# A LayerNorm-attention kernel: the first group in halves, x loaded ahead of the weights, a plain first slice, and two small moves in every group

**Chip, cores, metric.** One core of one Trainium2 chip. The metric is the device time of one execution in microseconds (us).

## The reference

128 graphs of 128 nodes with 768 features; 12 heads of 64; everything is fp32.

```python
h = jnp.maximum(_layernorm(x), 0.0)                       # no gain, no offset, eps 1e-5
q, k, v = (split_heads(h @ W + b) for W, b in ((Wq, bq), (Wk, bk), (Wv, bv)))
scores = jnp.einsum('bhqd,bhkd->bhqk', q, k) / 8
scores = scores + beta * adj[:, None]
scores = jnp.where(adj[:, None] > 0, scores, -9e15)
x = x + merge_heads(softmax(scores) @ v)
```

## The kernel before

It works in 32 groups of four graphs. In each group the three projections run as three "slices" (`qk0`, `v`, `qk1`). A slice multiplies a 2x3 by a 3x3 grid of blocks with 15 block products in place of 18. For that it needs sums of activation blocks (`S..`, 11 per group) and sums of weight blocks (`T..`, 15 per slice, once for the whole kernel). The 15 products write into four PSUM banks (chains a to d); a product that adds to a bank may not start until VectorE or ScalarE has taken the bank's last result out (an *eviction*).

The parts that the change and the argument touch, with cuts marked `# ...`:

```python
def load_x(G, g):                       # 4 DMAs on the sync queue
    # ...
        nc.sync.dma_start(t[a * SQ:(a + 1) * SQ], src[a])
for g in range(GRP):
    load_x(0, g)
# load_weights("qk0"): 18 DMAs on the scalar queue, at the same time
#     nc.scalar.dma_start(t[:, :, i * P:(i + 1) * P], part(w, oc * P, P))

def sum_weights(sl, n):                 # one T block
    # ... the two "-" sums: nc.vector.scalar_tensor_tensor
        e = nc.gpsimd if n % 3 == 2 else nc.vector
        e.tensor_tensor(wt[sl, name], wt[sl, a], wt[sl, b], ALU.add if sign > 0 else ALU.subtract)

def moments_2(G, mean, d):
    nc.tensor.matmul(pm[G][:, 1], mean8.rearrange("p a i -> p (a i)"), d, start=True, stop=True)
    nc.vector.tensor_reduce(ve, pm[G][:, 1], AX.X, ALU.add)
    nc.vector.tensor_scalar(ve, ve, EPS, None, op0=ALU.add)
    nc.gpsimd.tensor_tensor(rstd[G], ve, nhalf.to_broadcast([P, GRP * NB]), ALU.pow)
    nc.vector.scalar_tensor_tensor(shift[G], mean, -1.0, rstd[G], op0=ALU.mult, op1=ALU.mult)

def norm(G, g):                         # ScalarE: x <- relu(rstd * x + shift)
def to_hT(G, r, k):                     # VectorE transposes: one A block from x
def sum_acts(G, n):                     # one S block; every third on GpSimd

def make_bias(G, raw):
    # ... transpose, mask kp, a = min(beta*adj, cap)
    nc.gpsimd.tensor_tensor(t, a, a, ALU.mult)
    nc.vector.tensor_reduce(bm, t, AX.X, ALU.max)
    nc.vector.tensor_tensor(seen_b, seen_b, bm, ALU.max)
    nc.gpsimd.memset(t, MASKED)
    nc.vector.copy_predicated(t, kp, a)

# the eviction in slice v, in product():
    nc.vector.tensor_tensor(o4, bias..., p..., ALU.add)      # first into a v tile
    nc.vector.tensor_tensor(o, o, got, ALU.add)              # later ones

# the start: all of group 0's statistics, norm, transposes and sums, then the first product
moments_2(0, *moments_1(0))
for g in range(GRP): norm(0, g)
for n in HT_ORDER: to_hT(0, int(n[1]), int(n[2]))
for n in range(len(SUMS_A)):
    sum_acts(0, n); sum_weights("qk0", n)
# ... make_bias(0, a)
for G in range(NG):
    # group 0: the sums of v's weights under slice qk0, those of qk1 under slice v
    slice_of(G, "qk0", todo)
    # statistics, moments, bias and norm of group G+1 under slice v
    slice_of(G, "v", todo)
    # to_hT and sum_acts of group G+1, attention of group G under slice qk1
    slice_of(G, "qk1", todo)
```

## Time and profile before

| | before |
|---|---|
| time, median of 3 runs | 3209.32 us (3209.32 to 3209.43) |
| span of the profiled run, granted clock | 3208.3 us, 0.997 |
| TensorE busy | 3109.2 us, 97% |
| first product of slice qk0, of v, of qk1 in group 0 | 52.71, 82.71, 111.84 us |
| one group from the next (power to power) | 97.96 us |

TensorE is busy nearly all the time, so a change counts by the idle time it takes from TensorE. A row of the waits gives the engine that stood still, the tile and line it was about to work on, what it waited for, and then microseconds in all, number of times, longest. A row of the timeline gives start, length, engine, line, operation, output<-inputs, shape, count, and in brackets the idle time before it and what ended it. The lines themselves stand in the prediction. A product is four matmuls in the program; the trace records each of them as two, so a product is x8. Line numbers are those of each kernel's own text: the product is L305 before and L314 after.

### The profile page before, as it was taken

How to read it: one execution, taken by the hardware profiler on the slowest of the kernel's cores; microseconds unless marked ns; L12 is line 12 of the kernel's file. 1: busy time of each engine (PE TensorE's matmuls, PEld its weight loads, DVE VectorE, ACT ScalarE, POOL GpSimd, SP SyncE). 2: the span in 40 equal slices, each digit the busy share in tenths (PEclk: the TensorE clock that was granted, in tenths of full speed). 3: DMA queues.
4: the chain of work that ended last, by engine and by line, in shares of the span. 5: the costliest groups of instructions: out<-in, count | busy, mean ns of one | idle time of the engine just before them, and what ended most of it. 6: DMA issues, size and time to landing. Idle time of an engine off the chain costs nothing.

```text
span 3208.3 us, 46341 instructions
## 1 busy us (share of the span) xinstructions
PE 3109.2 (97%) x17794; PEld 2737.0 (85%) x17794; DVE 1962.6 (61%) x5031; ACT 781.5 (24%) x1665; POOL 571.2 (18%) x448
## 2 busy tenths in 40 slices
PE   3999999999999999999999999999999999999998
PEld 2888888888888888888888888888888888888887
DVE  6665566655666655666566666556665666665554
ACT  1222122222132221222221322222222213222221
POOL 3111111111111111111111111111111111111110
PEclk9999999999999999999999999999999999999998
DMA  6111121112111211211121112112111112121111
GB/s 153 43 52 45 53 63 46 53 43 56 53 54 49 54 43 53 63 47 53 45 55 53 55 48 56 41 53 63 47 53 46 54 53 56 47 56 37 50 40 31
DMA packets 358385, 169.94 MB, mean 53 GB/s; under 512 B 84368, under 2 KB 358032, under 8 KB 358160
## 3 DMA queue, kind: packets, MB, share of 16 engines
q1 hardware_dynamic: 344064, 159.45, 18.2%
q10 hardware_dynamic: 14096, 7.48, 0.9%
q8 instruction: 142, 2.33, 0.3%
q14 instruction: 83, 0.68, 0.1%
HBM read 116.53 MB, written 50.33 MB: 52 GB/s over the span
## 4 chain that ended last, share of the span: by engine, by line
PE 87%; DVE 5%; POOL 3%; issue 1%; DMA 1%; ACT 1%; ACTq 0%; POOLq 0%; DVEq 0%
PE pc_qk L305 18%; PE pb_qk L305 14%; PE pa_qk L305 14%; PE av L357 10%; PE pd_qk L305 7%; PE sc L344 7%; PE pb_v L305 5%; PE pc_v L305 5%; PE pa_v L305 3%; PE pd_v L305 3%; POOL rstd L243 3%; DVE A L258 2%; DVE v L321 2%; ACT x L251 1%; DMA v_B<-in_L_gnn_Wv_dram 0%
## 5 line engine op out<-in xcount | busy, mean ns | idle before, releaser
L251 ACT ACTIVATE x<-x,shift,rstd 128x192 f32<-128x192 f32 x512 | 227.8, 533 | 902.8 <-DVE shift L245 902.8
L348 ACT ACTIVATE e<-e 128x512 f32<-128x512 f32 x384 | 235.6, 630 | 819.9 <-DVE e L347 819.9
L368 POOL TENSOR_TENSOR xo<-xo,o 128x512 f32<-128x512 f32 x192 | 244.2, 1272 | 974.6 <-DVE seen L366 608.6
L357 PEld LDWEIGHTS av<-v,e 128*128 128x128 f32 x3072 | 375.4, 193 | 15.4 <-ACT e L348 5.4
L305 PE MATMUL pb_qk<-S,qk_T 128*128 128x256 f32 x1536 | 373.0, 386 | 0.5 <-DVE qk L330 0.5
L357 PE MATMUL av<-v,e 128*128 128x65 f32 x3072 | 367.0, 273 | 4.7 <-ACT e L348 4.7
L305 PEld LDWEIGHTS pb_qk<-S,qk_T 128*128 128x128 f32 x1536 | 281.7, 190 | 41.6 <-DVE qk L330 0.9
L347 DVE SCALAR_TENSOR_TENSOR e<-sc,biasT 128x512 f32<-128x512 f32 x384 | 246.6, 684 | 104.1 <-PE sc L344 104.1
L330 DVE TENSOR_TENSOR qk<-qk,pb_qk 128x512 f32<-128x512 f32 x256 | 174.4, 681 | 179.8 <-PE pb_qk L305 166.2
L326 ACT ACTIVATE qk<-pc_qk,bqk 128x256 f32<-128x256 f32 x384 | 160.9, 470 | 489.3 <-PE pc_qk L305 489.3
L258 DVE STREAM_TRANSPOSE A<-x 128x256 f32<-128x256 f32 x384 | 222.0, 618 | 77.7 <-ACT x L251 41.3
L305 PE MATMUL pc_qk<-S,qk_T 128*128 128x256 f32 x1024 | 243.8, 381 | 16.1 <-DVE S L264 16.1
L305 PE MATMUL pa_qk<-S,qk_T 128*128 128x256 f32 x1024 | 248.5, 385 | 0.0
L305 PE MATMUL pc_qk<-S,qk_B 128*128 128x256 f32 x1024 | 248.5, 385 | 0.0
L305 PEld LDWEIGHTS pc_qk<-S,qk_T 128*128 128x128 f32 x1024 | 195.6, 191 | 43.0 <-DVE S L264 16.2
L344 PE MATMUL sc<-qk 64*128 64x128 f32 x3072 | 224.4, 285 | 0.0
L305 PEld LDWEIGHTS pa_qk<-S,qk_T 128*128 128x128 f32 x1024 | 189.4, 190 | 30.8
L305 PEld LDWEIGHTS pc_qk<-S,qk_B 128*128 128x128 f32 x1024 | 189.4, 190 | 30.8
L344 PEld LDWEIGHTS sc<-qk 64*128 64x128 f32 x3072 | 187.1, 188 | 30.1 <-issue 21.2
L330 DVE TENSOR_TENSOR qk<-qk,pd_qk 128x512 f32<-128x512 f32 x128 | 88.0, 687 | 181.2 <-PE pd_qk L305 181.2
L264 POOL TENSOR_TENSOR S<-S,A 128x512 f32<-128x512 f32 x64 | 81.8, 1278 | 642.4 <-PE pa_qk L305 614.2
L305 PE MATMUL pb_v<-v_T,S 128*128 128x256 f32 x768 | 184.7, 383 | 5.4 <-DVE v L321 5.4
(106 smaller groups left out, 4647.2 us busy)
## 6 DMA issues: line engine op xcount, KB each, us to landing
x<-in_x_dram SPq DMA_DIRECT2D x512, 96.0 KB, 2.2
xo<-in_x_dram SPq DMA_DIRECT2D x192, 256.0 KB, 2.8
out_dram<-xo SPq DMA_DIRECT2D x192, 256.0 KB, 2.2
adj<-in_adj_dram SPq DMA_DIRECT2D x128, 64.0 KB, 2.3
qk_B<-in_L_gnn_Wq_dram ACTq DMA_DIRECT2D x18, 128.0 KB, 3.7
qk_B<-in_L_gnn_Wk_dram ACTq DMA_DIRECT2D x18, 128.0 KB, 3.6
v_B<-in_L_gnn_Wv_dram ACTq DMA_DIRECT2D x9, 256.0 KB, 5.9
bv_b<-in_L_gnn_bv_dram ACTq DMA_DIRECT2D x1, 384.0 KB, 4.7
```

The costliest lines, as they stand in the source:

```text
L243: nc.gpsimd.tensor_tensor(rstd[G], ve, nhalf.to_broadcast([P, GRP * NB]), ALU.pow)
L251: nc.scalar.activation(t, t, AF.Relu, bias=shift[G][:, n:n + 1], scale=rstd[G][:, n:n + 1])
L258: nc.vector.transpose(t[:, :, g * N:(g + 1) * N].rearrange("p c (b i) -> p c b i", i=SQ), src)
L264: e.tensor_tensor(t, A[G, a], A[G, b], ALU.add if sign > 0 else ALU.subtract)
L305: nc.tensor.matmul(p[:, i, :], lhs, rhs, start=(first and i == 0 and c == 0), stop=(c == 1), skip_group_check=True)
L326: nc.scalar.activation(t[:, i, :], p[:, i, :], AF.Identity, bias=bqk[:, i, oc:oc + 1], scale=float(sign))
L330: nc.vector.tensor_tensor(t, t, p, ALU.add if sign > 0 else ALU.subtract)
L344: nc.tensor.matmul(ps[i][:, g, :], t[r, 1, at], t[r, 0, at], start=True, stop=True)
L347: nc.vector.scalar_tensor_tensor(e, ps[i], SCORE_CAP * ISCALE, biasT[G], op0=ALU.min, op1=ALU.add)
L348: nc.scalar.activation(e, e, AF.Exp, scale=1.0 / ISCALE)
L357: nc.tensor.matmul(pa[:, 2 * g + i, :], es[G, oc, i][:, 2 * r + g, :], vt[G, "v", r, h // 4][:, 4 * g + h % 4, :], start=True, stop=True)
L368: nc.gpsimd.tensor_add(t, t, o.rearrange("p a (b j) d -> p (a b) (j d)", j=2))
```

## The change

Its intent: let TensorE start as soon as half of x is there, and make the block sums while it already works. Group 0 is treated in two halves; x is loaded first on two queues and the weights behind it; slice qk0 of group 0 is computed plainly with 18 products, which needs no sums; the sums of v and qk1 are to be made under it, and those of qk0 (for the groups after, all but two of them on GpSimd) under slice v. In all groups the LayerNorm shift moves from VectorE to GpSimd (with a mean already negative), and the bias is made in two steps, so that VectorE need not wait for GpSimd's square.

The diff, cut to its core (left out: a new order of the weight sums, five of which now overwrite a raw weight block, and a few small loads and scalings on other queues):

```diff
-            nc.sync.dma_start(t[a * SQ:(a + 1) * SQ], src[a])
+            engines[a % len(engines)].dma_start(t[a * SQ:(a + 1) * SQ], src[a])
-        load_x(0, g)
+        load_x(0, g, (nc.sync, nc.scalar))
-    nc.vector.tensor_scalar(mean8, ..., 0.125, None, op0=ALU.mult)
+    made = nc.vector.tensor_scalar(mean8, ..., -0.125, None, op0=ALU.mult)
-                nc.scalar.dma_start(t[:, :, i * P:(i + 1) * P], part(w, oc * P, P))
+                nc.sync.dma_start(t[:, :, i * P:(i + 1) * P], part(w, oc * P, P))
 # moments_2 (now over blocks lo to hi of the group)
-        nc.vector.scalar_tensor_tensor(shift[G], mean, -1.0, rstd[G], op0=ALU.mult, op1=ALU.mult)
+        shifted = nc.gpsimd.tensor_tensor(t, mean, r, ALU.mult)
 # bias_1
-        nc.gpsimd.tensor_tensor(t, a, a, ALU.mult)
-        ... tensor_reduce(bm, t, ...), tensor_tensor(seen_b, seen_b, bm, ALU.max)
         nc.gpsimd.memset(t, MASKED)
         nc.vector.copy_predicated(t, kp, a)
+        nc.gpsimd.tensor_tensor(a, a, a, ALU.mult)
+    def bias_2(G, a):
+        ... tensor_reduce(bm, a, ...), tensor_tensor(seen_b, seen_b, bm, ALU.max)
+    def plain_slice(G, sl, todo):        # 6 blocks x 3 products of raw A and B blocks
+    def after(f, *args):                 # queue behind the last transpose / the last shift
+        with tc.issue_after(first["dve"].ins), tc.issue_after(first["pool"].ins):
+            return f(*args)
+    with tc.issue_after(made.ins):
+        for step in range(3):
+            half(0, step)                # statistics, moments, norm, transposes of half 0
 # loop, group 0
+            with tc.issue_after(first["dve"].ins):
+                half(1, 0)
+            then(1, lambda: half(1, 1))
+            then(3, lambda: half(1, 2))
+            for n in range(len(SUMS_A)):
+                then(n + 5, lambda n=n: after(sum_acts, 0, n))
+            for n in range(len(SUMS_B)):
+                then(n // 2 + 5, lambda n=n: after(sum_weights, "v", n))
+                then(n // 3 + 13, lambda n=n: after(sum_weights, "qk1", n))
+            then(9, lambda: bias_2(0, after(bias_1, 0, adj_0)))
+            plain_slice(0, "qk0", todo)
 # under slice v of group 0
+                then(n, lambda n=n: after(sum_weights, "qk0", n, nc.gpsimd))
```

## The prediction

> **What bounds the kernel now.** I read the page first, then the waits of TensorE, the chain of work in order of time, and the timeline of the start and of one later group. TensorE is the bound: it is busy in nearly all of the span, so only its idle time and its extra matmuls count.
>
> ```profile
> PE 3109.2 (97%) x17794; PEld 2737.0 (85%) x17794; DVE 1962.6 (61%) x5031; ACT 781.5 (24%) x1665; POOL 571.2 (18%) x448
> ...
> PE pm L227 <- DVE st L219: 31.9, 1, 31.9
> PE pa_v L305 <- DVE v L321: 27.1, 31, 0.9
> PE pc_qk L305 <- DVE S L264: 16.1, 1, 16.1
> PE pb_v L305 <- DVE v L321: 5.4, 31, 0.2
> PE pm L238 <- DVE dev L233: 3.5, 1, 3.5
> ```
>
> Waits are in us: total, times, longest. Two stocks are on offer. One is the start: three waits that occur once, 31.9 + 3.5 + 16.1 = 51.5 us. The other recurs in each of 31 groups: 27.1 + 5.4 = 32.5 us. If the change won both, 84 us would be 2.6%.
>
> The recurring wait, in the timeline of a late group (start, length, engine, ...):
>
> ```profile
> 2549.95 2.90 POOL L243 TENSOR_TENSOR rstd<-ve,nhalf 128x16 f32<-128x16 f32 x1 [16.23 <-DVE ve L241]
> 2552.89 0.17 DVE L245 SCALAR_TENSOR_TENSOR shift<-mean,rstd 128x16 f32<-128x16 f32 x1 [3.08 <-POOL rstd L243]
> 2553.10 7.12 ACT L251 ACTIVATE x<-x,shift,rstd 128x192 f32<-128x192 f32 x16 [28.65 <-DVE shift L245]
> 2554.99 1.17 DVE L258 STREAM_TRANSPOSE A<-x 128x256 f32<-128x256 f32 x2 [1.33 <-ACT x L251]
> 2556.78 1.99 PE L305 MATMUL pa_v<-v_B,S 128*128 128x256 f32 x8 [0.88 <-DVE v L321]
> ```
>
> The power on GpSimd, then the shift, then four norm instructions on ScalarE, then two transposes on VectorE, which stand in VectorE's queue ahead of the eviction that TensorE needs.
>
> The start, in the chain of work (start, length, what):
>
> ```profile
> 52.71 3.78 PE pc_qk L305 x8
> 56.49 2.35 PE pa_qk L305 x8
> 58.84 1.73 PE pb_qk L305 x8
> ...
> 88.81 1.99 PE pc_v L305 x8
> ...
> 111.84 1.73 PE pc_qk L305 x8
> ```
>
> A product is four matmuls, 1.73 us when warm. The first slice starts at 52.71. At 88.81 stands the fourth product of the second slice (v), at 111.84 the first of the third (qk1). From there on both kernels have the same TensorE order; the rest lasts 3208.3 - 111.8 = 3096.5 us.
>
> **What the Trainium skill says.** "SBUF — State Buffer", section "SBUF: two separate sides": VectorE and GpSimd share a port pair, an exclusive lock held for a whole instruction, which a VectorE operation with two SBUF inputs needs against a GpSimd operation that reads SBUF; the other blocks. The trace agrees:
>
> ```profile
> 34.15 1.75 POOL L198 TENSOR_TENSOR v_T<-v_T,v_B 128x512 f32<-128x512 f32 x1 [2.23 <-DVE v_T L198]
> 34.69 1.25 DVE L233 SCALAR_TENSOR_TENSOR dev<-st,dev 128x32 f32<-128x32 f32 x1
> ...
> 50.84 2.94 POOL L264 TENSOR_TENSOR S<-A,A 128x512 f32<-128x512 f32 x2 [6.52 <-DVE A L258]
> 51.72 3.21 DVE L264 TENSOR_TENSOR S<-A,A 128x512 f32<-128x512 f32 x3
> ```
>
> A 128x32 operation, 0.2 us elsewhere, lasts 1.25 and ends with the sum on GpSimd. In the second pair five sums last from 50.84 to 54.93, 4.09 us, close to 2 x 1.27 + 3 x 0.6 = 4.3: one at a time, taking turns. "TensorE: Matmul & The Clock Gate", Part 1: after an idle window of some 3.4 us the array runs at half clock, and warms in about that time. The trace agrees: 3.78 and 2.35 after 16 us of idle, so 3.78 + 2.35 - 2 x 1.73 = 2.67 us lost. "GPSIMD Engine Reference", section 3.1: a GpSimd tensor_tensor of 2048 elements takes 4497 ns; with 1270 ns for 512 in this trace I estimate a fixed part of 0.2 us.
>
> **The change part by part.**
>
> 1. *x ahead of the weights, on two queues.* Before, both streams share the DMA engines, and the last x piece lands at 29. The 2 us stretches show 241 to 269 GB/s from 2 to 14 us. The first half of x is 0.79 MB: at 250 GB/s from about 1.7 us, landed at about 5. Two batches of statistics on VectorE (1.1 each) end at 6.3. Then the moments: matmul 0.65, four small operations 0.9, matmul 0.65, two small 0.5, the power. The power took 2.9 for 16 columns; for 8 I take 1.6. Shift on GpSimd 0.3. Norm of two batches 3.6 (16 took 7.12), last transpose 0.6. Sum: TensorE starts at 15.5 instead of 52.7. The weights follow from 6 us, 2.36 MB at 250 GB/s, and stay ahead of it.
>
> 2. *Plain first slice.* 18 products for 15: 18 x 1.73 + 2.67 cold + 0.3 for moments = 34.1, so it ends at 49.6. Its tenth product needs the second half of x. The built order puts that half's moment matmuls after products 2 and 4 (21.7 and 25.2); then 0.5 + 1.6 + 0.3 + 3.6 + 0.6 gives 32.0, and TensorE asks at 34. It fits, by 2 us.
>
> 3. *The sums under it.* This is where I think the gain goes. Before, the sums of two weight slices and of the activations ran while TensorE waited anyhow. Now nearly all three slices' sums stand in VectorE's and GpSimd's queues after the last transpose, at 33, and the built order has 31 VectorE sums and the bias work *ahead of* the first eviction of slice v. Among them two wait for GpSimd; the later, T1 of qk1, for the twentieth GpSimd operation after that time. The lock makes these additive: 20 GpSimd operations x 1.13 (1.27 less what is dispatched while waiting) = 22.6, VectorE's 27 sums x 0.55 and four others 1.5 = 16.3, from 33.8: 72.7. Then three more sums, one or two GpSimd turns, three statistics and the eviction, 4.5 to 5.5: 78. TensorE gets through three products of slice v (49.6 + 5.2 = 54.8) and then stands still, because the fourth adds to the bank that the eviction must read first. That is a wait of about 23 us, and long enough to go cold: another 2.67.
>
> So the fourth product starts at 78 instead of 88.8. The rest of the slice took 111.8 - 88.8 = 23.0 before; with the cold start 25.7, and perhaps 0.7 for the bias of the next group, which now stands between its last evictions: qk1 starts at 104.5 instead of 111.8. Gain: 7.3 us.
>
> 4. *Shift on GpSimd, negative mean.* In the built order each later group is the same on TensorE and VectorE except for the shift and the bias steps. VectorE no longer waits for the power, but it was idle for another 1.33 us afterwards for ScalarE, so nothing is released: the transposes still wait for norm, norm for shift, shift for the power. Before, 0.25 us pass from the power's end to ScalarE's start; with a GpSimd shift of 0.2 and two hand-overs about 0.3. Cost: 31 x 0.08 = 2.5 us.
>
> 5. *Bias in two steps.* It takes a 1.15 us wait of VectorE for GpSimd out of each group. TensorE does not wait there: 0.
>
> Sum: 3209.3 - 7.3 + 2.5 = 3204.5. I put 3203, as the rivals below weigh on the fast side.
>
> **Rivals.** (a) *The sums hide.* Were there no lock, VectorE would reach the eviction at 33 + 31 x 0.6 + 4.1 = 56, TensorE would wait 2 us, and qk1 would start near 79: a gain of 30 us, 3180. For it speaks that the order was evidently chosen so; against it the two pairs above. In between, VectorE may win the lock more often, yet it still has to wait for those 20 GpSimd operations. (b) *The recurring wait goes*, 32.5 us more: 3170 or, with (a), 3147. Against it: the 1.33 us of waiting for ScalarE after the shift, and an unchanged order. (c) *The shift on GpSimd is slow*, or the small power is not cheaper: 0.3 us per group is 9 us, and a power of 2.9 for 8 columns moves part 1 by 1.3 and the sums with it by 2.6. Then 3212. (d) The second half of x is late: a few us inside the first slice, which the wait at the fourth product would absorb.
>
> **Range and chances.** The firm limit is the start: with everything hidden 37.2 - 5.2 = 32 us, 1.0%. To be faster by 2% (64 us) needs (a) and (b) together, which I hold for nearly excluded; slower by 2% would need 2 us lost in every group, and nothing in the order does that. The low end, 3187, is two thirds of the way to (a); the high end, 3212, is (c).
>
> **What would show it.** Right: the first product at 15 to 17 us; in slice v of group 0 one TensorE wait of 18 to 26 us for an eviction (v), with VectorE and GpSimd busy in turns beneath it and VectorE sums of 1.6 us instead of 0.68; the wait of pa_v for v still 31 times 0.9; steady groups 97.97 to 98.1 us apart, as before (power to power). Wrong: no such wait (the lock costs less than I think), a recurring wait gone, or groups closer together than 97.9.

## The result, and the profile after

The changed kernel is correct and took 3204.72 us (median of 4, 3204.31 to 3205.04), against 3209.38 us (4 runs) of the kernel before on the same chip. The ratio is 0.9985 with a 95% interval of 0.9968 to 1.0002: the same within 2%. A ratio is the mean time of one kernel's fast runs over that of the other's fast runs of the same rounds, so it is not quite the ratio of the medians.

| | before | after |
|---|---|---|
| span of the profiled run, clock | 3208.3 us, 0.997 | 3203.1 us, 0.993 |
| first product of group 0 | 52.71 | 16.92 |
| first product of slice v | 82.71 | 50.62 |
| first product of slice qk1 | 111.84 | 103.82 |
| from there to the end of the span | 3096.5 | 3099.3 |
| power to power | 97.96 | 98.05 |

TensorE starts 35.8 us earlier and reaches slice qk1 only 8.0 us earlier; then it loses 2.8 us in the rest. The page of the kernel after, TensorE's busy time:

```profile
PE 3115.6 (97%) x17822; PEld 2743.3 (86%) x17822; DVE 1963.9 (61%) x4988; ACT 781.2 (24%) x1665; POOL 590.1 (18%) x489
```

It is 6.4 us busier than before, of which three more products at 1.73 us are 5.2. TensorE's waits in the kernel after:

```profile
PE pa_v L314 <- DVE v L330: 29.6, 31, 1.0
PE pc_v L314 <- DVE v L325: 23.5, 1, 23.5
PE pm L227 <- DVE st L218: 7.9, 1, 7.9
PE plain L404 <- DVE A L263: 6.9, 1, 6.9
PE pb_v L314 <- DVE v L330: 5.1, 30, 0.2
```

The three single waits of the start (51.5 us) have become 7.9 + 6.9 + 0.9 us, and one new wait of 23.5 us stands in slice v. The recurring pair has grown from 32.5 to 34.7 us. The timeline has TensorE's first product of the kernel after:

```profile
16.92 5.79 PE L404 MATMUL plain<-A,qk_T 128*128 128x256 f32 x16 [6.86 <-DVE A L263]
```

The chain of work of the kernel after, around the new wait and at the start of qk1:

```profile
77.89 0.79 DVE st L218 x3
78.68 0.60 DVE v L325
79.42 3.53 PE pc_v L314 x8
82.94 1.73 PE pd_v L314 x8
...
103.82 1.73 PE pc_qk L314 x8
```

The fourth product of slice v starts at 79.42, as soon as VectorE has got to the eviction (v) at 78.68; it runs at half clock (3.53 for 1.73 us). What VectorE and GpSimd did until then, in the timeline of the kernel after:

```profile
52.19 0.68 DVE L270 TENSOR_TENSOR S<-A,S 128x512 f32<-128x512 f32 x1
...
61.21 1.59 POOL L198 TENSOR_TENSOR qk_T<-qk_T,qk_T 128x512 f32<-128x512 f32 x1
61.60 1.74 DVE L270 TENSOR_TENSOR S<-A,S 128x512 f32<-128x512 f32 x1
62.76 1.70 POOL L198 TENSOR_TENSOR qk_T<-qk_T,qk_B 128x512 f32<-128x512 f32 x1
63.27 1.75 DVE L198 TENSOR_TENSOR qk_T<-qk_T,qk_B 128x512 f32<-128x512 f32 x1
```

The sum at 52.19 has VectorE to itself and lasts 0.68 us. From 61 us on each engine's operation starts before the other's has ended and cannot finish until it has: 1.74 and 1.70 us, with 1.67 us from one VectorE sum to the next (61.60 to 63.27). That is what the prediction expected to see. Last, a late group of the kernel after, which answers to the five lines of before:

```profile
2543.91 2.91 POOL L245 TENSOR_TENSOR rstd<-ve,nhalf 128x16 f32<-128x16 f32 x1 [16.17 <-DVE ve L243]
2546.90 0.22 POOL L247 TENSOR_TENSOR shift<-mean,rstd 128x16 f32<-128x16 f32 x1
2547.16 7.12 ACT L256 ACTIVATE x<-x,shift,rstd 128x192 f32<-128x192 f32 x16 [28.75 <-POOL shift L247]
2549.05 1.15 DVE L263 STREAM_TRANSPOSE A<-x 128x256 f32<-128x256 f32 x2 [3.64 <-ACT x L256]
2550.13 0.64 DVE L330 TENSOR_TENSOR v<-v,pa_v 128x512 f32<-128x512 f32 x1
2550.82 1.99 PE L314 MATMUL pa_v<-v_B,S 128*128 128x256 f32 x8 [0.96 <-DVE v L330]
```

VectorE's wait of 3.08 us for the power is gone, but its wait ahead of the transposes has grown from 1.33 to 3.64 us. The order is the same; the hand-over over GpSimd takes 3.25 us from the power's start to ScalarE's (2543.91 to 2547.16), before it was 3.15 (2549.95 to 2553.10).

### The profile page after: what moved, and what is told of

It reads as the page before. It is cut to its first block, busy times and chain, and to the rows that moved or that the text cites. A ratio compares the mean times of both kernels' runs of the same rounds, so it can differ in the third digit from the quotient of the medians.

```text
span 3203.1 us, 46402 instructions
## 1 busy us (share of the span) xinstructions
PE 3115.6 (97%) x17822; PEld 2743.3 (86%) x17822; DVE 1963.9 (61%) x4988; ACT 781.2 (24%) x1665; POOL 590.1 (18%) x489
## 4 chain that ended last, share of the span: by engine, by line
PE 87%; DVE 6%; POOL 3%; issue 2%; ACT 1%; DMA 1%; SPq 1%; ACTq 0%; POOLq 0%; DVEq 0%
PE pc_qk L314 17%; PE pb_qk L314 14%; PE pa_qk L314 14%; PE av L366 10%; PE pd_qk L314 7%; PE sc L353 7%; PE pb_v L314 5%; PE pc_v L314 5%; PE pa_v L314 4%; PE pd_v L314 3%; POOL rstd L245 3%; DVE A L263 2%; DVE v L330 2%; ACT x L256 1%; SPq L180 0%
## 5 line engine op out<-in xcount | busy, mean ns | idle before, releaser
L356 DVE SCALAR_TENSOR_TENSOR e<-sc,biasT 128x512 f32<-128x512 f32 x384 | 246.5, 683 | 104.0 <-PE sc L353 103.8
L339 DVE TENSOR_TENSOR qk<-qk,pd_qk 128x512 f32<-128x512 f32 x126 | 86.6, 687 | 178.1 <-PE pd_qk L314 178.1
L245 POOL TENSOR_TENSOR rstd<-ve,nhalf 128x16 f32<-128x16 f32 (+1 forms) x33 | 93.4, 2830 | 524.6 <-DVE ve L243 524.6
```

What stands on the lines that cost most here:

```text
L245: nc.gpsimd.tensor_tensor(r, ve, nhalf.to_broadcast([P, n]), ALU.pow)
L339: nc.vector.tensor_tensor(t, t, p, ALU.add if sign > 0 else ALU.subtract)
L356: nc.vector.scalar_tensor_tensor(e, ps[i], SCORE_CAP * ISCALE, biasT[G], op0=ALU.min, op1=ALU.add)
```

## The experiments

Twelve kernels ran, all correct. The kernel before took 3209.4 to 3211.8 us (medians) on the chips that they shared, so times are compared as ratios, and differences under some 5 us (the width of an interval to one side) are read from the profile. One caution for such readings: the last attention block, with the same instructions, took 2.4 us longer in one profile (all_dve) than in another (the kernel after), and 3.3 us longer in that of both_late, so spans carry an error of that size, while the starts of stages and the distance of groups hardly do (a few profiles have one single group of 98.3 us among the 98.05).

| run | base | time, us | ratio to before [95%] | fourth product of v starts | group to group |
|---|---|---|---|---|---|
| the change | | 3204.72 | 0.9985 [0.9968, 1.0002] | 79.4 | 98.05 |
| all_dve | after | 3189.65 | 0.9933 [0.9918, 0.9949] | 61.6 | 98.05 |
| idle_tt | after | 3207.79 | 0.9990 [0.9973, 1.0007] | 78.8 | 98.05 |
| idle_memset | after | 3190.13 | 0.9934 [0.9917, 0.9950] | 62.3 | 98.05 |
| pool_late | after | 3205.04 | 0.9982 [0.9967, 0.9997] | 68.4 | 98.05 |
| qk1_late | after | 3192.89 | 0.9943 [0.9927, 0.9960] | 67.1 | 98.05 |
| both_late | after | 3197.01 | 0.9953 [0.9936, 0.9970] | 58.5 | 98.05 |
| hT_behind | after | 3153.26 | 0.9823 [0.9806, 0.9839] | 78.8 | 96.38 |
| shift_dve | after | 3202.22 | 0.9972 [0.9959, 0.9986] | 78.3 | 97.96 |
| bias_one | after | 3206.69 | 0.9986 [0.9971, 1.0001] | 79.3 | 98.05 |
| x_first_only | before | 3195.90 | 0.9952 [0.9935, 0.9969] | | 97.96 |
| best | after | 3148.22 | 0.9802 [0.9786, 0.9819] | 58.9 | 96.38 |
| best2 | after | 3140.85 | 0.9781 [0.9764, 0.9797] | 62.3 | 96.38 |

"Fourth product" means in each row the first one that adds to a bank of slice v that must be evicted first. (In the four kernels with all sums on VectorE the scheduler put another product, into the still free bank d, ahead of it.)

### What holds the eviction up: turns at a lock, or the sums themselves?

**all_dve.** Take GpSimd's share of the first group's sums away and give it to VectorE.

```diff
-            e = e or (nc.gpsimd if n % 3 == 2 else nc.vector)
+            e = nc.vector
-        e = nc.gpsimd if n % 3 == 1 else nc.vector
+        e = nc.gpsimd if n % 3 == 1 and G else nc.vector
```

> The changed kernel with every sum of the first group (weights and activations) on VectorE and none on GpSimd. If the lock makes the two engines take turns, giving GpSimd nothing costs VectorE little: its sums fall from 1.75 us to about 0.6 each, the fourth product of slice v starts at about 63, qk1 at about 90, total about 3191. Rival: without a lock the moved sums lengthen VectorE's queue, the eviction comes later (about 84) and the whole is some 5 us slower, 3210.

The wait list and the timeline of this kernel:

```profile
PE pc_v L314 <- DVE v L325: 5.0, 1, 5.0
```

```profile
60.85 0.68 DVE L325 TENSOR_TENSOR v<-bv_b,pc_v 128x512 f32<-128x512 f32 x1
...
61.59 3.78 PE L314 MATMUL pc_v<-v_T,S 128*128 128x256 f32 x8 [4.98 <-DVE v L325]
```

VectorE does more work and reaches the eviction 17.8 us earlier (60.85 for 78.68 us). The 23.5 us wait is down to 5.0. The theory said 63 and 3191; 61.6 and 3189.65 were measured. (Its start of qk1, about 90, can't be compared: the scheduler pulled qk1's first product into slice v, to 79.7; the second starts at 86.6.) The no-lock rival (84, 3210) is out. But this alone does not exclude that VectorE had waited for *results* of GpSimd. The next two runs separate these.

**idle_tt** and **idle_memset.** As all_dve, with identical order on VectorE and TensorE in both; GpSimd works on a scratch tile that nobody reads.

```diff
+    scratch = work.tile([P, 2, 4, HD], F32, tag="o", name="scratch", bufs=2)
+    def busy():
+        nc.gpsimd.tensor_tensor(scratch, scratch, scratch, ALU.add)    # idle_tt
+        for _ in range(3): nc.gpsimd.memset(scratch, 0.0)              # idle_memset
+            # called wherever GpSimd had a sum
-        nc.gpsimd.tensor_tensor(a, a, a, ALU.mult)
+        (nc.gpsimd if G else nc.vector).tensor_tensor(a, a, a, ALU.mult)
```

> As the kernel with all sums on VectorE, but GpSimd adds a scratch tile to itself (128x512) 25 times from about 29 us on; nobody reads that tile, and the bias square of the first group is on VectorE so that nothing waits for GpSimd. If it is the lock that costs, some 21 of these fall under VectorE's 45 operations, at 1.67 - 0.6 = 1.07 us for each: the eviction slips from 61 to about 84, the fourth product follows it, total about 3211. Rival: VectorE was late because it waited for sums that GpSimd delivered; here it needs none, so the eviction stays at 61 to 62 and the total at 3188.

> The control: same order on VectorE and TensorE, but GpSimd writes its scratch tile 75 times (memset, 0.48 us from one to the next, some 36 us in all) in place of the 25 additions. It reads nothing of SBUF. If the lock is one of operations that read on both sides, VectorE keeps its 0.6 us per sum, the eviction stays at 61 to 62 and the total at about 3188. Rival: any work on GpSimd slows VectorE (or memory in general); then the eviction slips by 10 us or more here too.

The timeline of idle_tt, and then that of idle_memset, at the same stage:

```profile
49.23 13.85 POOL L206 TENSOR_TENSOR scratch<-scratch 128x512 f32<-128x512 f32 x10
...
51.07 1.52 DVE L280 TENSOR_TENSOR S<-S,A 128x512 f32<-128x512 f32 x1
```

```profile
49.89 14.49 POOL L207 MEMSET scratch<- 128x512 f32 x25
...
51.91 0.68 DVE L194 SCALAR_TENSOR_TENSOR qk_T<-qk_B,qk_B 128x512 f32<-128x512 f32 x1
```

Useless additions on GpSimd bring the wait back: the eviction slips from 61.5 to 78.1 us, and the time from 0.9934 to 0.9990. Even more microseconds of writing on GpSimd leave the sums alone: 0.68 us per sum, eviction at 61.5. In neither does VectorE stand idle for a result of GpSimd in this stretch, and its operations come in the same order. So the cause is the contention of two engines that both read SBUF (the memory in which the operands of both lie here). The size was off: I expected 84 and 3211. An addition of a tile to itself gave turns of 1.45 us and not 1.67, so 0.85 us and not 1.07 were lost for each; the trace has 19 VectorE operations lengthened in this way, and 19 x 0.85 is 16.2 of the 16.5 us.

**pool_late.** The 13 GpSimd sums for qk0, needed only from group 1 on, go behind the shift of group 1.

```diff
-                then(n, lambda n=n: after(sum_weights, "qk0", n, nc.gpsimd))     # under slice v
+            with tc.issue_after(first["shift"].ins):                            # under slice qk1
+                after(sum_weights, "qk0", n, nc.gpsimd)
```

> The changed kernel with the 13 GpSimd sums of the weights of qk0 (needed only from the second group on) issued after the shift of group 1 instead of inside slice v of group 0. If the alternating turns at the lock are what delays the eviction, some 8 of these GpSimd turns fall away under it at 1.13 us each: the wait of slice v shrinks from 23.5 to about 14 us, the fourth product starts at about 70 instead of 79.4, total about 3195.5. Rival: only the length of VectorE's own queue counts, whatever GpSimd does; then the wait stays 23.5 and the time 3204.7.

The wait at the fourth product fell to 13.2 us (14 was expected), and the product starts at 68.4. But the time did not move. The timeline of VectorE in this kernel shows where the gain went:

```profile
91.52 1.74 DVE L194 SCALAR_TENSOR_TENSOR qk_T<-qk_T,qk_B 128x512 f32<-128x512 f32 x1 [6.03 <-POOL qk_T L198]
...
103.59 0.69 DVE L295 TENSOR_REDUCE bm<-adjT 128x4 f32<-128x512 f32 x1 [4.68 <-POOL adjT L290]
```

The first is one of the two sums of qk0 that stay on VectorE: it overwrites a raw block and so waits until a moved GpSimd sum has read it (90.20 to 91.48). The second waits for the square of group 1's bias, which stands in GpSimd's queue behind moved sums. Behind them in VectorE's queue stand evictions of slice v, and TensorE waits 6.0 and 2.7 us more, at half clock afterwards. My edit moved the sums to a bad place; as a test of the wait it worked, as a remedy it did not.

**qk1_late.** The sums of qk1 stand behind the evictions of slice v instead of ahead of the first.

```diff
-                then(n // 3 + 13, lambda n=n: after(sum_weights, "qk1", n))
+                then(n, lambda n=n: behind(sum_weights, "qk1", n))    # slice v; behind: issue_after(last eviction)
```

> The changed kernel with the sums of qk1's weights on VectorE and GpSimd issued in slice v, each behind the eviction of a product, instead of ahead of the first eviction of slice v. Theory: the eviction stands behind work that is not needed for 50 us more. Moved behind it, the fourth product of slice v starts at about 61 to 65 instead of 79.4. The sums then fall due in slice v and qk1, whose start gains less: about 96, total about 3197. Rival: the queue ahead of the eviction is set by the sums of v, which are needed anyway; then the wait shrinks by under 5 us.

The product starts at 67.1, slice qk1 at 91.4 in place of 103.8, and it took 3192.89 us. That is 2 us later at the product and 5 us earlier at qk1 than expected; the rival (under 5 us) is out. So it also helps to put the same work where it is not in the way. (Four of the fifteen moved sums are GpSimd's, so part of the gain is fewer turns ahead of the eviction; this run does not split the two.)

**both_late.** The two edits together.

> The sums of qk1 behind the evictions of slice v and the GpSimd sums of qk0 behind the shift of group 1, together. Theory: nearly all of the 23.5 us wait goes, and little comes back: qk1 starts at 86 to 88 instead of 103.8, total about 3188. Rival: the work comes back as waits in slice v or qk1 and the total stays above 3197.

The wait is down to 3.4 us, the product starts at 58.5 and qk1 at 83.5 (86 to 88 was expected), but the time is no better than with qk1_late alone: behind qk1's first product TensorE now waits 8.9 us for an eviction that stands in VectorE's queue behind a wait of 10.8 us for the square of group 1's bias, the same trap as in pool_late. The rival was nearly right (3197.0, "above 3197").

### What is behind the recurring wait

**hT_behind.** In every group the transposes of the next group stand behind the last eviction of slice v in VectorE's queue.

```diff
-                    nc.vector.tensor_tensor(o, o, got, ...)
+                    ev[0] = nc.vector.tensor_tensor(o, o, got, ...)
-                then(at, lambda n=n: to_hT(G + 1, int(n[1]), int(n[2])))
+                then(at, lambda n=n: behind(to_hT, G + 1, int(n[1]), int(n[2])))   # issue_after(ev[0])
```

> The changed kernel with the transposes of the next group behind the last eviction of slice v in VectorE's queue, in every group. The recurring wait (29.6 us of pa_v and 5.1 of pb_v for that eviction) is said to come from two transposes that stand ahead of it and wait for power, shift and norm. If so, both waits vanish: about 34 us faster, 3170, and 1.1 us less from power to power. Rival: the eviction is late for another reason, or the transposes, now later, make the next group's sums late; then the time stays within 5 us of 3204.7, or is worse, with a wait of equal size in the qk1 slice.

The late group in the timeline of this kernel:

```profile
2507.55 1.89 PE L314 MATMUL pa_v<-v_B,S 128*128 128x256 f32 x8
...
2509.28 1.89 PE L314 MATMUL pb_v<-v_T,S 128*128 128x256 f32 x8
...
2511.81 1.15 DVE L263 STREAM_TRANSPOSE A<-x 128x256 f32<-128x256 f32 x2
```

Both waits are gone from the list, in all groups, and nothing came back. The groups are 96.38 us apart, 1.67 us closer, and 31 x 1.67 = 51.8 us agrees with the times (3204.72 to 3153.26, on two chips). So the cause was right and the size wrong: I had expected 34 us, the sum of the waits. Set the starts of the products of the two late groups side by side: all stages are equal but three. From pc_v to pa_v it is 2.85 us with the wait and 1.73 without, from pa_v to pb_v 2.17 and 1.73, from pb_v to pc_qk 1.83 and 1.73: 1.12 + 0.44 + 0.10 = 1.66. The list gives 0.96 + 0.18. The rest has two parts that the list cannot show. The matmul before a wait is drawn to its own end, while in an undisturbed stream the next one starts 0.16 us before that; and the second matmul after a wait starts 0.32 us after the first and not 0.22, as its weights are loaded late. That makes some 0.26 us for each stop.

### The two small moves, and the parts of the start

**shift_dve.** Shift back on VectorE.

```diff
-        shifted = nc.gpsimd.tensor_tensor(t, mean, r, ALU.mult)
+        nc.vector.tensor_tensor(t, mean, r, ALU.mult)
```

> The changed kernel with the shift back on VectorE (mean already negative, so a plain product). My theory: the shift on GpSimd is what lengthens each of 31 groups by 0.07 to 0.08 us, because the power, the norm on ScalarE and the transposes still follow one another. So power to power goes back from 98.05 to 97.97, the wait of pa_v for the eviction from 1.0 to 0.9, and the whole is about 2.4 us faster than the changed kernel (about 3202.3). Rival: the move to GpSimd freed VectorE from a 3 us wait and was worth something elsewhere; then this kernel is slower than the changed one by more than 1 us.

Groups are 97.96 us apart again, and pa_v waits 26.9 us in all instead of 29.6. The timeline of a late group in this kernel:

```profile
2543.12 0.17 DVE L247 TENSOR_TENSOR shift<-mean,rstd 128x16 f32<-128x16 f32 x1 [3.08 <-POOL rstd L245]
...
2545.22 1.16 DVE L263 STREAM_TRANSPOSE A<-x 128x256 f32<-128x256 f32 x2 [1.33 <-ACT x L256]
```

So GpSimd's shift costs 31 x 0.09 = 2.7 us and frees nothing. The intervals of the two ratios (0.9972 and 0.9985) overlap; the distance of the groups is constant to 0.03 us in both kernels.

**bias_one.** The bias in one step, as before.

```diff
+        nc.gpsimd.tensor_tensor(t, a, a, ALU.mult)
+        ... tensor_reduce(bm, t, ...), tensor_tensor(seen_b, seen_b, bm, ALU.max)
         nc.gpsimd.memset(t, MASKED)
         nc.vector.copy_predicated(t, kp, a)
-        nc.gpsimd.tensor_tensor(a, a, a, ALU.mult)
```

> The changed kernel with the bias made in one step again: the square on GpSimd into the bias tile, the maximum right behind it, then the masking. My theory: VectorE waits about 1.15 us more in each group for GpSimd, at a place where TensorE does not wait for it, so the time stays within 0.5 us of the changed kernel (3204.7). Rival: the two steps are worth the 1.15 us in each of 31 groups; then it is up to 35 us slower.

The groups stay 98.05 us apart and the ratio is 0.9986 for 0.9985. The profiled run reached qk1 of group 0 some 1.5 us later; 0.5 us can't be told apart in the time. The step is worth nothing in the later groups. It also takes out less of VectorE's wait than was thought: 1.17 us in each group with one step, and still 0.59 with two.

**x_first_only.** The kernel before with its loads changed and nothing else.

```diff
-            nc.sync.dma_start(t[a * SQ:(a + 1) * SQ], src[a])
+            engines[a % len(engines)].dma_start(t[a * SQ:(a + 1) * SQ], src[a])   # group 0: sync, scalar
-                nc.scalar.dma_start(t[:, :, i * P:(i + 1) * P], part(w, oc * P, P))
+                nc.sync.dma_start(t[:, :, i * P:(i + 1) * P], part(w, oc * P, P))
```

> The kernel before with only the loads changed: x first on two queues, the weights after it on one. Theory: of the three parts of the new start (loads, half of x at a time, plain slice) the loads alone move the moments from 31.9 us of waiting to about 10, so that the first product starts at 33 to 38 instead of 52.7, and since all sums are made before it, none is given back: total about 3190 to 3195, more gain than the whole change. Rival: the weights, now later, delay their own sums by as much as x is earlier, the start stays near 50 and the time near 3207.

The timeline of this kernel:

```profile
34.93 3.78 PE L305 MATMUL pc_qk<-S,qk_T 128*128 128x256 f32 x8 [18.55 <-DVE S L264]
```

The first product starts 17.8 us earlier and qk1 at 97.8 instead of 111.8, so 3.8 us are given back after all (one wait of 4.3 us for an eviction on ScalarE), and the time, 3195.9, is just above what was expected. By these starts and by the ratio (0.9952 for 0.9985) the loads alone give more than the whole change: the halves and the plain slice take TensorE another 18 us ahead (16.92), and the three products more and the sums under them lose more than that again.

### Together

**best**: both_late, hT_behind and shift_dve. **best2**: all_dve, hT_behind and shift_dve.

> The four edits together: sums of qk1 and of qk0 late, transposes behind the last eviction, shift on VectorE. If the causes are separate, the gains add: 3204.7 - 17 - 34 - 0 to 2 = about 3152. If they share a cause the total is over 3165.

> All sums of the first group on VectorE, the transposes of the next group behind the last eviction, the shift on VectorE. If the three causes are separate: 3187.6 - 31 x 1.66 (the whole cost of the recurring wait) - 0 to 2.5 = about 3134 to 3136, some 2.3% under the kernel before. Rival: the gains overlap, and it stays above 3145.

best was 4 us better than expected, by errors of both signs: hT_behind brought 18 us more than its estimate, both_late some 8 less, and the other 6 went into waits of TensorE in group 0 (4.0, 2.8, 1.2 and 1.2 us) and half clock after them. Its verdict is unclear (the interval contains 0.98). best2 is faster than the kernel before by 2.2%, and its interval lies below 0.98; it is the best version that I found. Its span, 3138.6, is 3 to 5 us above the estimate: hT_behind makes the shift's place irrelevant in the later groups (96.38 with either), and a wait of 2.4 us for an eviction appears in slice v of group 0 that all_dve did not have. The timeline of VectorE in best2 shows where it comes from:

```profile
84.33 0.18 DVE L247 TENSOR_TENSOR shift<-mean,rstd 128x16 f32<-128x16 f32 x1 [3.43 <-POOL rstd L245]
```

Back on VectorE, the shift waits 3.43 us for the power, and the eviction stands behind it (85.02). TensorE loses 2.4 us waiting and another 1.7 in the next product, at half clock. So shift_dve, worth something on its own, seems to cost some 4 us in this company; best2 with the shift left on GpSimd was not run. TensorE is busy for 3101.8 of 3138.6 us.

## Why the prediction was right

3203 was predicted and 3204.7 measured, inside 3187 to 3212. By its own steps:

1. *Start at 15.5.* Measured 16.92. The term that was off is the landing of the second x batch: its statistics began at 6.75 and ended at 7.9, not 6.3. The chain from there took 9.0 us. The prediction allowed 9.2 for it; the terms that it lists add up to 8.8 only, so the written sum has 0.4 us that no term accounts for. The power of 8 columns took 1.64 us (1.6) and the shift 0.20 (0.3).
2. *Plain slice, end at 49.6.* Slice v starts at 50.62, so the slice took 33.7 us (34.1). The second half's transposes ended at 34.4, not 32.0; TensorE did not wait for them.
3. *Wait of 23 us, fourth product at 78, qk1 at 104.5.* Measured 23.5, 79.4 and 103.8: a gain of 8.0 us for 7.3. The mechanism, turns at the lock, is shown by idle_tt against idle_memset. At the steps that they take alone (0.60 us for a sum), VectorE's operations from 34.27 to 78.60 would last 21.4 us; they took 44.3, so 22.9 went to turns, for the 22.6 of the prediction. VectorE was never idle there: the prediction let it wait for GpSimd's results, but the turns alone make the time. The cold clock, a term of this step, cost less than the 2.67 us assumed: 3.53 - 1.73 = 1.8. That the end agrees to 0.7 us is partly luck: the product came 1.4 us later than predicted, and the rest of the slice took 24.4 us for 26.4.
4. *0.08 us per group for the shift.* Measured 0.09, and shift_dve takes it away.
5. *Bias: 0.* bias_one agrees within what can be told apart, though the wait was halved (1.14 to 0.59 us in each group) and not taken out.

The sum of the steps was 3204.5; the number on record, 3203, had been lowered for rivals that did not come true.

Of the rivals, (a), that the sums would hide, was wrong for this kernel. Its estimate of the eviction without a lock (56) was in the right region, though it takes the sums off GpSimd and not better luck at the lock: all_dve has it at 61 although VectorE does everything. (b), that the recurring wait goes, did not come true, for the reason given (the order of the queue). What failed in this part is its stock: "27.1 + 5.4 = 32.5" is the sum of the listed waits, while removing them was worth 52 us in the kernel after, and would be worth 31 x (97.96 - 96.38) = 49 us in the kernel before (worked out from the distances of the groups, not run). The statement that both stocks together are 84 us or 2.6% was thus too low by some 16 us; it did not touch the predicted time, as the change left that wait alone. (c) did not occur; (d) did, by 2.4 us, and cost nothing.

What stays open: I did not run a version that keeps the plain slice and leaves GpSimd with only some of the sums, so the best split is not known; nor one that joins best2's edits to the kernel before with only x loaded first; nor best2 with the shift on GpSimd.

## What to carry to other kernels

Two engines that share a lock don't add up: here a 128x512 sum given to GpSimd cost VectorE 1.07 us, more than the 0.6 us it takes to do that sum itself, so "offloading" lengthened the queue ahead of the eviction that TensorE needed. Before taking an early start, list what stands in each in-order queue ahead of the first thing the bound engine will ask for; an order edit (transposes behind the last eviction) was worth ten times the whole change. And count a recurring short stop by comparing starts with an undisturbed stretch: the listed idle time was only two thirds of its cost.

## What the Trainium skill lacked or had wrong

- "SBUF — State Buffer", "Who interferes with whom", has the rule right as far as these runs show: VectorE sums with two SBUF inputs were held up by GpSimd additions (1.52 us) and not by its memsets (0.68 us). It lacks what two full queues make of the lock: turns, 1.67 us from one VectorE sum to the next where one alone takes 0.60.
- "TensorE: Matmul & The Clock Gate", Part 1, gives the window of some 3.4 us, calls it free-running, and says that what is issued in the first 3.4 us or so after idling runs at half clock (by my estimate from that, 1.7 us lost). As the size of a single stop this is too narrow: 5.0 us of idle time cost 2.84 us in the next two products (all_dve: 3.57 + 2.73 from start to start, for 2 x 1.73), while 23.5 us of it cost 1.6 to 1.8 (after). The granted clock (PEclk) in the two traces shows why: it is half until 67.19 us in all_dve, 5.6 us after the restart at 61.59, and until 82.58 in the kernel after, 3.2 us after the restart at 79.42. Half of these is 2.8 and 1.6, so the loss went with the moment at which the clock came back and not with the length of the stop, which fits a free-running window.
- The same Part 1 has half clock follow an idle window of some 3.4 us. Here less was enough: in best2 TensorE waited 2.40 us and the clock was half from 85.71 to 89.12 us; in pool_late it waited 2.72 us and the clock was half from 105.11 to 108.52.
- "GPSIMD Engine Reference", section 3.1, has the addition but not the power: 2.91 us for 128x16 and 1.64 us for 128x8.
- What a short stop of TensorE costs beyond its listed idle time, I found as a figure on none of the pages that I read: 0.96 + 0.18 us listed, 1.66 us lost.
